# A hand-made order for the first block of a layernorm, attention and routed-FFN kernel

## The chip, the cores and the metric

The kernel runs on one core of one Trainium2 chip. The metric is the time of one execution on the device in microseconds (us). TensorE (PE, with its weight loads PEld), VectorE (DVE), ScalarE (ACT), GpSimd (POOL) and SyncE (SP, which here only issues DMAs) each work through a queue of their own, in order, and wait for one another by semaphores.

## The reference

```python
xn = layernorm(x)                                  # x: 2 x 2048 x 2048, float32
qkv = xn @ Wqkv + bqkv                             # three of 512
attn = softmax(q @ k.T / sqrt(512)) @ v @ Wo + bo
scores = (xn @ Wq.T) @ keys.T                      # 64 experts, 16 kept
gate = one_hot(top16) weighted by softmax(top16)
ffn = ((xn @ A.T) * gate, each 8 times) @ B.T * 2
out = x + attn + ffn
```

## The kernel before, in words

The 4096 tokens are 8 blocks of T = 512, each 4 token tiles of 128. Products are made to near float32 accuracy from a high and a low half: ACT casts a value to its high half (`split_hi`, L127), DVE or POOL subtracts it from the value (`split_lo`, L130), and three matmuls (`PASSES`) make one product. From the second block on, products are formed for pairs of blocks with fewer multiplications, from sums of quarters of the weights ("P1" to "P7"). These sums are made once by POOL (`four_sums`, L541 to L544: four additions), stored to DRAM (`sq_d`, `sv_d`) and read back later. For the feature weights 0 and 2 they are whole tiles of 1024 columns (`set_load`, `set_sums`, `set_out`); for 4, 1, 3 and 5 eight half tiles of 512 columns, called parts (`part_load`, `part_sums`, `part_out`; tile hs, L1169 and L1178). The tables `beside_F` and `beside_V` say behind which step of the features and of the values each part is loaded (L), summed (S_) and stored (O).

`first_block` (from about L320) does the first block's layernorm and its values and router columns (528, in two halves of VH = 264). For each token tile: two rows of x of 1024 columns are loaded (L333); DVE takes statistics (`normal`: L225, L228, L341, L218), POOL the power that gives the reciprocal deviation rs (L219); DVE scales three quarters (L349) and ACT one (L353, L354); PE transposes 16 chunks of 128 x 128 in four groups of four (`turn`, L363), each group into a PSUM bank (acc0, acc1, acc2, acc6); ACT and DVE split the chunks one by one into xh (16 casts, 16 subtractions). Eight weight pieces wh (128 x 2 x 264) are cast on ACT; pieces 2 to 4 are subtracted on POOL, the others on DVE. The sums of token tile t lie in bank acc(3 + t), 48 matmuls each (`mul`, six for each of 8 steps c2). Then `values_out` splits the results into vs and `flush` stores them (L170). In the second half the other 264 columns follow, four banks at once, and beside them the row statistics of the next block (`stats_steps`, whose x rows ACT's queue loads, L243). Then come the features (`features`, 12 weight pieces pw through `fetch`, L622), the values of the second block (`values_by_half`, "Q" and "R"), `third`, and the phases. `whole` (L1140) adds the halves of xh again.

What is issued when is mostly left to a scheduler, which goes by due times; `behind(...)` (`issue_after`) holds an instruction behind named ones.

Of the kernel before, what the change touches and what calls it, by code (L numbers as in the profile page):

```python
# [62 lines left out]
def attn_ffn_kernel(ctx: ExitStack, tc, x, xT, wq, wv, wob, bqk, bv, bo, keysT, out):  # L63
# [114 lines left out]
    XH0 = [s for n in range(3) for s in (GROUPS[3][n + 1], T_SLOTS[n])] + [26, T_SLOTS[3]]  # L178
    XH1 = [s for n in range(3) for s in (GROUPS[2][n + 1], T_SLOTS[4 + n])] + [None, T_SLOTS[7]]

    def split_room(at):
        if at is None:
            return [half(k)([P, T], FR, "xh") for k in (7, 8)]
        t = big(at)([P, 2, T], FR, "xh")
        return [t[:, k, :] for k in range(2)]
# [45 lines left out]
    def stats_steps(i, r, cols, out):  # L231
# [13 lines left out]
        def rows(k):  # L245
            t, c = divmod(k, per)
            if k == 0:
                v["mv"] = const.tile([P, NT, 2], F32, name="mv", bufs=2)
                for n in range(len(r.tags) - 2):
                    load(n)  # L250
# [24 lines left out]

        return [lambda k=k: rows(k) for k in range(NT * per)] + [chain, spread_out]

    mbs = {}
# [40 lines left out]
    def first_block(steps):  # L319
# [3 lines left out]
        xn = [split_room(at) for at in XH0 + XH1]  # L323
        rows, mv = {}, const.tile([P, NT, 2], F32, name="mv", bufs=2)
        rs = const.tile([P, NT], F32, name="rs")
        nm = const.tile([P, NT], F32, name="nm")

# [9 lines left out]

        def normal(t):
            st = const.tile([P, 4, 6], F32, name="st6", bufs=2)
            row_stats(mv[:, t, :], rows[t], 0, st)  # L340
            last["nm"] = nc.vector.tensor_scalar(nm[:, t : t + 1], mv[:, t, 0:1], -1.0, None, ALU.mult)  # L341
            rstd(rs[:, t : t + 1], mv[:, t, 1:2], 1)

        def scale(t):
            for n in range(4):
                c, h = divmod(n, 2)
                v = rows[t][c][:, h * 512 : (h + 1) * 512]
                if n < 3:
                    last["row"] = nc.vector.tensor_scalar(  # L349
                        v, v, mv[:, t, 0:1], rs[:, t : t + 1], ALU.subtract, ALU.mult  # L350
                    )
                else:
                    nc.scalar.activation(v, v, AF.Identity, bias=nm[:, t : t + 1])  # L353
                    last["mul"] = nc.scalar.mul(v, v, rs[:, t : t + 1])  # L354

        def turn(t, g0=0, g1=NCH // 4):
            sl = slice(t * P, (t + 1) * P)
            for g in range(g0, g1):
                pt = acc((0, 1, 2, 6)[g])
                for j in range(4):  # L360
                    c = 4 * g + j
                    k = (c % 8) * P
                    nc.tensor.transpose(pt[:, j * P : (j + 1) * P], rows[t][c // 8][:, k : k + P], ident)  # L363
                for part in range(2):
                    for j in range(4):
                        hi, lo = (xn[4 * g + j][a][:, sl] for a in range(2))
                        pj = pt[:, j * P : (j + 1) * P]
                        if part == 0:
                            split_hi(hi, pj)
                        else:  # L370
                            last["row"] = split_lo(lo, pj, hi)

        r_w0 = Ring(sb, "h0", "h1", "h2", "h3", "B25", "B34", "B35", "B32")

        def mul(ps, wh, t, c2):
            sl = slice(t * P, (t + 1) * P)
            for cc in range(2):
                c = 2 * c2 + cc
                product(
                    ps[:, :VH], lambda a: xn[c][a][:, sl], lambda b: wh[:, b, cc, :],  # L380
                    c == 0, c == NCH - 1,
                )
# [5 lines left out]
        for j in range(25):  # L388
            nc.tensor.matmul(pw, warm[:, :P], warm, start=True, stop=True)
        load(0, 512)  # L390
        normal(0)
        scale(0)

        wh = []

        def piece():
            wh.append(wv_hi(0, len(wh), r_w0))

        def low(n):
            with behind("row", "nm", "mul"):  # L400
                wh[n] = weights_lo(*wh[n], nc.gpsimd if 2 <= n < 5 else None)

        piece()
        piece()
        low(0)
        low(1)
        piece()
        turn(0, 0, 2)
        low(2)
        piece()  # L410
        turn(0, 2, 4)
        low(3)
        piece()
        low(4)
        load(1, 1024)
        for n in range(5, N2):
            piece()
        with behind("row"):
            normal(1)
        with behind("nm"):  # L420
            low(5)
        load(2, 1024)
        ps = []
        for t in range(NT):
            ps.append(acc(3 + t))
            for c2 in range(N2):
                if t + 1 < NT and c2 == 2:
                    scale(t + 1)
                    if t + 2 < NT:
                        with behind("row"):  # L430
                            normal(t + 2)
                if t == 0 and c2 == 4:
                    low(6)
                    low(7)
                    load(3, 1024)
                    constants()
                if t + 1 < NT and c2 == 6:
                    with behind("pe"):
                        turn(t + 1)
                mul(ps[t], wh[c2], t, c2)  # L440
        qr = router_in()
        for t in range(NT):
            with behind("row"):
# [4 lines left out]
        for c2 in range(N2):  # L448
            w = wv_piece(1, c2)
            if c2 == N2 - 1:  # L450
                fetch(0)
            for t in range(NT):
                mul(ps[t], w, t, c2)
# [6 lines left out]
        return xn, qr  # L460
# [77 lines left out]
    def four_sums(w00, w01, w10, w11):  # L538
# [1344 lines left out]
```

## Time and profile before

| | us |
|---|---|
| timed runs: lowest, median, highest of 3 | 2580.51, 2582.38, 2585.69 |
| the profiled execution, span from first to last instruction (the page gives no other time of it) | 2582.2 |
| PE busy in the span | 2556.8 |
| first block, first half: first transposes to the last sum of the fourth token tile | 9.29 to 47.60 |
| first block, second half | 47.60 to 70.83 |
| features | 70.83 to about 137 |
| values of the second block and what follows, up to the last step that the change touches | about 137 to 270 |

A busy share is read together with what ended each idle stretch: the view of waits names who waited for whom, and the timeline gives each instruction's start, its length, and in brackets the idle time before it and who released it. The windows give the busy time of each engine between two moments.

### The profile page before, as it was taken

The numbers are of one execution on the slowest core, as the hardware profiler recorded it, in microseconds if no ns is written. First come the engines' busy times: TensorE is split into PE (matmuls) and PEld (weight loads), VectorE is DVE, ScalarE is ACT, GpSimd is POOL, SyncE is SP. The second block draws the span as 40 slices with busy tenths as digits, with TensorE's granted clock in tenths as the row PEclk, the third lists the DMA queues.
The fourth block names the chain that finished last, engine by engine and source line by source line (L and its number), as shares of the span: only waits on it lengthen the run. The fifth ranks groups of instructions, "written<-read, shape, count | busy, mean of one in ns | idle before, by whom it ended". The sixth has DMA issues, their size and how long they took to land. (4 is left out here: it accounts for less than half of the span.)

```text
span 2582.2 us, 34227 instructions
## 1 busy us (share of the span) xinstructions
PE 2556.8 (99%) x12546; PEld 2159.7 (84%) x12546; DVE 1981.2 (77%) x2692; ACT 926.9 (36%) x1327; POOL 560.8 (22%) x340
## 2 busy tenths in 40 slices
PE   9999999999999999999999999999999999999999
PEld 8897888888888889888887878878878888888887
DVE  7788997867778678777668768688597777797675
ACT  4333333232332323343345446354364222332221
POOL 2382310001000000000000000000013565576654
PEclk9999999999999999999999999999999999999999
DMA  8988964668356673678899798898897554665552
GB/s 297 311 300 276 354 224 144 227 212 274 125 176 225 211 250 120 201 269 270 315 310 309 240 338 278 282 324 290 277 320 265 182 162 157 203 200 179 167 168 101
DMA packets 334297, 615.41 MB, mean 238 GB/s; under 512 B 28409, under 2 KB 151345, under 8 KB 334129
## 3 DMA queue, kind: packets, MB, share of 16 engines
q1 hardware_dynamic: 318864, 583.33, 67.2%
q10 hardware_dynamic: 15264, 29.89, 3.3%
q8 instruction: 99, 1.62, 0.3%
q14 instruction: 70, 0.57, 0.1%
HBM read 457.76 MB, written 155.35 MB: 237 GB/s over the span
## 5 line engine op out<-in xcount | busy, mean ns | idle before, releaser
L135 PE MATMUL acc<-t,pw 128*128 128x512 f32 x3744 | 859.0, 390 | 6.4 <-DVE t L130 4.7
L135 PEld LDWEIGHTS acc<-t,pw 128*128 128x128 f32 x3744 | 699.8, 188 | 153.9 <-DVE t L130 6.4
L1629 PE MATMUL acc<-wb,s 128*128 128x512 f32 x2688 | 609.6, 389 | 0.0
L1629 PEld LDWEIGHTS acc<-wb,s 128*128 128x128 f32 x2688 | 504.4, 188 | 105.0 <-DVE s L130 0.2
L1613 POOL TENSOR_TENSOR xo<-xo,bo_bc 128x512 f32<-128x512 f32 x128 | 213.5, 1675 | 884.5 <-DMA bo_bc<-in_bo 592.3
L127 ACT CAST pw<-pw 128x1024 fp32r<-128x1024 f32 (+1 forms) x218 | 230.5, 1058 | 442.1 <-PE acc L135 287.8
L135 PE MATMUL acc<-ph,vt 128*128 128x512 f32 x1536 | 376.7, 390 | 0.3 <-ACT ot L1474 0.2
L130 DVE TENSOR_TENSOR pw<-pw 128x1024 fp32r<-128x1024 f32 (+1 forms) x218 | 288.7, 1324 | 95.9 <-ACT pw L127 94.3
L135 PEld LDWEIGHTS acc<-ph,vt 128*128 128x128 f32 x1536 | 287.7, 188 | 62.1 <-issue 1.2
L1335 PE MATMUL acc<-qt,kt 128*128 128x512 f32 x1344 | 333.9, 390 | 2.6 <-ACT sp L1345 1.5
L1335 PEld LDWEIGHTS acc<-qt,kt 128*128 128x128 f32 x1344 | 250.9, 188 | 58.9 <-DVE qt L130 2.2
L135 PE MATMUL acc<-pw,t 128*128 128x264 f32 x2400 | 295.9, 285 | 2.9 <-DVE pw L130 0.9
L135 PEld LDWEIGHTS acc<-pw,t 128*128 128x128 f32 x2400 | 294.2, 189 | 5.3 <-ACT pw L127 1.1
L127 ACT CAST s<-xz 128x1024 fp32r<-128x1024 f32 x112 | 118.0, 1054 | 375.1 <-PE acc L1629 300.3
L130 DVE TENSOR_TENSOR s<-xz,s 128x1024 fp32r<-128x1024 f32 x112 | 177.8, 1589 | 41.0 <-ACT s L127 41.0
L130 DVE TENSOR_TENSOR t<-xq,t 128x1024 fp32r<-128x1024 f32 x108 | 141.9, 1321 | 24.3 <-ACT t L127 24.1
L535 POOL TENSOR_TENSOR zt<-zt,g 128x512 f32<-128x512 f32 x28 | 44.6, 1603 | 516.0 <-DMA g<-gd 274.6
L127 ACT CAST t<-xq 128x1024 fp32r<-128x1024 f32 x108 | 113.1, 1051 | 114.1 <-DVE xq L667 59.6
L1618 DVE TENSOR_TENSOR xo<-xo,acc 128x512 f32<-128x512 f32 x128 | 86.9, 680 | 52.1 <-POOL xo L1659 25.2
L127 ACT CAST ph<-sp 128x512 fp32r<-128x512 f32 x128 | 79.4, 620 | 109.4 <-PE acc L135 108.5
L1654 POOL TENSOR_TENSOR xo<-xo,u 128x512 f32<-128x512 f32 x64 | 111.5, 1772 | 21.5 <-DVE u L1652 21.4
L225 DVE BATCH_NORM_STATS2 st<-xs 128x6 f32<-128x512 f32 x128 | 85.0, 683 | 39.5 <-DMA xs<-in_x 39.2
(174 smaller groups left out, 2229.4 us busy)
## 6 DMA issues: line engine op xcount, KB each, us to landing
vt<-v_d SPq DMA_DIRECT2D x128, 512.0 KB, 5.4
kt<-kp_d SPq DMA_DIRECT2D x224, 256.0 KB, 5.7
pw<-sq_d SPq DMA_DIRECT2D x96, 512.0 KB, 4.3
pw<-in_wq SPq DMA_DIRECT2D x72, 512.0 KB, 3.7
xo<-in_x SPq DMA_DIRECT2D x128, 256.0 KB, 3.0
xz<-oz_d SPq DMA_DIRECT2D x64, 512.0 KB, 4.4
out_y<-xo SPq DMA_DIRECT2D x128, 256.0 KB, 2.6
xq<-in_xT SPq DMA_DIRECT2D x56, 512.0 KB, 5.1
```

What stands on the lines that cost most here:

```text
L127: return nc.scalar.copy(hi, src)
L130: return (eng or nc.vector).tensor_tensor(lo, src, raw(hi), ALU.subtract)
L135: last["pe"] = nc.tensor.matmul(ps, st(a_), mv(b_), start=first and n == 0, stop=end and n == 2, skip_group_check=more,)
L225: nc.vector.bn_stats(st[:, parts, :], xt[:, h * 512 : (h + 1) * 512])
L535: nc.gpsimd.tensor_tensor(zt, zt, gx[n], ALU.mult)
L1335: last["pe"] = nc.tensor.matmul(ps, st[:, d, a, :], mv[c][:, d, :], start=not more and d == 0 and i == 0, stop=d == 1 and i == 2, skip_gro ...
L1613: nc.gpsimd.tensor_tensor(xs, xs, bo_bc[q // (NB // 2 * NH), c], ALU.add)
L1618: nc.vector.tensor_tensor(xs, xs, ps, op)
L1629: nc.tensor.matmul(ps, st[a_][:, kk, sl], mv[b_], start=not more and kk == 0 and n == 0, stop=kk == ND - 1 and n == 2, skip_group_check=more,)
L1654: nc.gpsimd.tensor_tensor(xo[q, t, a, 1], xo[q, t, a, 1], v, ALU.add)
```

## The change

The first half of the first block gets a fixed order on each of PE, DVE, ACT and POOL: every instruction issued through `inline` is held behind the one before it on its engine. Within that order: high and low halves of two chunks now share a tile (`pair_rooms` in place of `split_room`), so that one cast and one subtraction treat two chunks (the last pair's low halves stay apart, in two subtractions); each group of transposes is followed by its splits and by a weight cast; weight piece 5 is subtracted on POOL; the fourth group of transposes goes to the bank misc instead of acc6; the transposes of the next tile come one step (six matmuls) later; the three matmuls of a product run in reversed order. The first two parts are loaded behind the last rows of x (`part_load`), summed on POOL between the powers, three sums, three and two, and stored (`part_out`); the tables for the other parts move up by two. The next block's first two rows of x are loaded at the second token tile (`early`). In the second half, the casts and subtractions of four weight pieces come ahead of the results of token tiles 2 and 3. `whole` adds both chunks of a pair at once. `at` gives a chunk of a pair to the matmuls.

```diff
+        early[i] = lambda: [load(n) for n in range(len(r.tags) - 2)]
...
+        tail = {}
+        def inline(key, f, *a, **k):
+            if key in tail:
+                with tc.issue_after(tail[key].ins):
+                    tail[key] = f(*a, **k)
+            else:
+                tail[key] = f(*a, **k)
+            return tail[key]
+        dve = lambda f, *a: inline("dve", f, *a)
+        act = lambda f, *a, **k: inline("act", f, *a, **k)
+        pe = lambda f, *a, **k: inline("pe", f, *a, **k)
+        pool = lambda f, *a: inline("pool", f, *a)
...
         def normal(t):
-            st = const.tile([P, 4, 6], F32, name="st6", bufs=2)
-            row_stats(mv[:, t, :], rows[t], 0, st)
-            last["nm"] = nc.vector.tensor_scalar(nm[:, t : t + 1], mv[:, t, 0:1], -1.0, None, ALU.mult)
-            rstd(rs[:, t : t + 1], mv[:, t, 1:2], 1)
+            dve(nc.vector.bn_aggr, mv[:, t, :], parts[t])
+            ve = const.tile([P, NT], F32, name="ve", bufs=2)
+            dve(nc.vector.tensor_scalar, ve[:, :1], mv[:, t, 1:2], EPS, None, ALU.add)
+            pool(nc.gpsimd.tensor_tensor, rs[:, t : t + 1], ve[:, :1], nhalf[:, :1], ALU.pow)
+            dve(nc.vector.tensor_scalar, nm[:, t : t + 1], mv[:, t, 0:1], -1.0, None, ALU.mult)
...
-        def turn(t, g0=0, g1=NCH // 4):
+                    act(nc.scalar.activation, v, v, AF.Identity, bias=nm[:, t : t + 1])
+                    act(nc.scalar.mul, v, v, rs[:, t : t + 1])
+        turned = {}
+        def turn(t, g):
+            pt = turned[t, g] = acc(g) if g < 3 else misc()
+            for j in range(4):
+                c = 4 * g + j
+                k = (c % 8) * P
+                pe(nc.tensor.transpose, pt[:, j * P : (j + 1) * P], rows[t][c // 8][:, k : k + P], ident)
+        def sides(t, g, part):
             sl = slice(t * P, (t + 1) * P)
-            for g in range(g0, g1):
-                pt = acc((0, 1, 2, 6)[g])
...
-                for part in range(2):
-                    for j in range(4):
-                        hi, lo = (xn[4 * g + j][a][:, sl] for a in range(2))
-                        pj = pt[:, j * P : (j + 1) * P]
-                        if part == 0:
-                            split_hi(hi, pj)
-                        else:
-                            last["row"] = split_lo(lo, pj, hi)
+            for cp in (2 * g, 2 * g + 1):
+                src = turned[t, g][:, (cp % 2) * 2 * P : (cp % 2 + 1) * 2 * P]
+                src = src.rearrange("p (k t) -> p k t", k=2)
+                hi, lo = xn[cp]
+                if part == 0:
+                    act(split_hi, hi[:, :, sl], src)
+                elif isinstance(lo, list):
+                    for k in range(2):
+                        dve(split_lo, lo[k][:, sl], src[:, k, :], hi[:, k, sl])
+                else:
+                    dve(split_lo, lo[:, :, sl], src, hi[:, :, sl])
...
         def mul(ps, wh, t, c2):
             sl = slice(t * P, (t + 1) * P)
             for cc in range(2):
                 c = 2 * c2 + cc
-                product(
-                    ps[:, :VH], lambda a: xn[c][a][:, sl], lambda b: wh[:, b, cc, :],
-                    c == 0, c == NCH - 1,
-                )
+                for n, (a, b) in enumerate(PASSES[::-1]):
+                    pe(
+                        nc.tensor.matmul, ps[:, :VH], at(c, a)[:, sl], wh[:, b, cc, :],
+                        start=c == 0 and n == 0, stop=c == NCH - 1 and n == 2,
+                    )
...
+        def wload(n):
+            for k in range(n):
+                h, cc = divmod(2 * len(ws), HC)
+                ws.append(r_w0([P, 2, VH], F32, "ws"))
+                nc.sync.dma_start(ws[-1], wv[0, h, :, cc : cc + 2, :])
+        def high():
+            n = len(wh)
+            wh.append(r_wh([P, 2, 2, VH], FR, "wh"))
+            last["hi"] = act(split_hi, wh[n][:, 0], ws[n])
+        def low(n):
+            if n in (2, 3, 4, 5):
+                pool(nc.gpsimd.tensor_tensor, wh[n][:, 1], ws[n], raw(wh[n][:, 0]), ALU.subtract)
+            else:
+                dve(split_lo, wh[n][:, 1], ws[n], wh[n][:, 0])
+        wload(5)
+        load(1, 1024)
+        wload(3)
+        load(2, 1024)
+        load(3, 1024)
+        for n in range(2):
+            part_load(n)
...
         normal(0)
+        high()
         scale(0)
...
-        def low(n):
-            with behind("row", "nm", "mul"):
-                wh[n] = weights_lo(*wh[n], nc.gpsimd if 2 <= n < 5 else None)
-        piece()
-        piece()
+        high()
         low(0)
         low(1)
-        piece()
-        turn(0, 0, 2)
-        low(2)
-        piece()
-        turn(0, 2, 4)
-        low(3)
-        piece()
-        low(4)
-        load(1, 1024)
-        for n in range(5, N2):
-            piece()
-        with behind("row"):
-            normal(1)
-        with behind("nm"):
-            low(5)
-        load(2, 1024)
-        ps = []
+        for g in range(4):
+            turn(0, g)
+            sides(0, g, 0)
+            sides(0, g, 1)
+            high()
+            low(2 + g)
+        high()
+        high()
+        stats(1, 0)
+        stats(1, 1)
+        normal(1)
+        low(6)
+        low(7)
+        scale(1)
+        constants()
+        add = lambda *a: pool(nc.gpsimd.tensor_tensor, *a)
+        adds = [ad for n in range(2) for ad in part_adds(n, add)]
+        for ad in adds[:3]:
+            ad()
+        ws1 = []
+        def second_half():
+            h, cc = divmod(2 * len(ws1), HC)
+            ws1.append(r_ws([P, 2, VH], F32, "ws"))
+            last["sp"] = nc.sync.dma_start(ws1[-1], wv[1, h, :, cc : cc + 2, :])
+        for n in range(4):
+            second_half()
+        ps = [acc(3 + t) for t in range(NT)]
         for t in range(NT):
-            ps.append(acc(3 + t))
+            if t == 1:
+                early[1]()
             for c2 in range(N2):
-                if t + 1 < NT and c2 == 2:
-                    scale(t + 1)
+                if t + 1 < NT and c2 == N2 - 1:
+                    for g in range(4):
+                        turn(t + 1, g)
                     if t + 2 < NT:
-                        with behind("row"):
-                            normal(t + 2)
-                if t == 0 and c2 == 4:
-                    low(6)
-                    low(7)
-                    load(3, 1024)
-                    constants()
-                if t + 1 < NT and c2 == 6:
-                    with behind("pe"):
-                        turn(t + 1)
+                        stats(t + 2, 0)
+                    for g in range(3):
+                        sides(t + 1, g, 0)
+                        sides(t + 1, g, 1)
+                    sides(t + 1, 3, 0)
+                    if t + 2 < NT:
+                        stats(t + 2, 1)
+                        normal(t + 2)
+                    sides(t + 1, 3, 1)
+                    if t + 2 < NT:
+                        scale(t + 2)
+                        for ad in (adds[3:6], adds[6:])[t]:
+                            ad()
+                        part_out(t)
                 mul(ps[t], wh[c2], t, c2)
+        last["row"], last["pe"], last["mul"] = tail["dve"], tail["pe"], tail["act"]
         qr = router_in()
-        for t in range(NT):
-            with behind("row"):
+        for t in range(2):
+            with behind("row", "mul"):
+                values_out(0, t, 0, r_ev, qr, ps[t])
+        ahead = []
+        def lead():
+            n = len(ahead)
+            if n < N2:
+                if n + 4 > len(ws1) and len(ws1) < N2:
+                    second_half()
+                w = r_wh([P, 2, 2, VH], FR, "wh")
+                with behind("row", "mul"):
+                    last["hi"] = split_hi(w[:, 0], ws1[n])
+                    last["dve"] = split_lo(w[:, 1], ws1[n], w[:, 0])
+                ahead.append(w)
+        for n in range(4):
+            lead()
+        for t in range(2, NT):
+            with behind("row", "mul"):
                 values_out(0, t, 0, r_ev, qr, ps[t])
         flush()
...
-            w = wv_piece(1, c2)
+            lead()
             if c2 == N2 - 1:
                 fetch(0)
             for t in range(NT):
-                mul(ps[t], w, t, c2)
+                mul(ps[t], ahead[c2], t, c2)
+            last["pe"] = tail["pe"]
...
+    def four_adds(w00, w01, w10, w11, tt=None):
+        tt = tt or nc.gpsimd.tensor_tensor
+        return (w11, w00, w10, w01), [
+            lambda: tt(w11, w10, w11, ALU.add),
+            lambda: tt(w10, w00, w10, ALU.subtract),
+            lambda: tt(w00, w11, w00, ALU.subtract),
+            lambda: tt(w01, w01, w00, ALU.subtract),
+        ]
...
-    RINGS = (0, 0, 2, 1, 0, 2, 1, 0)
+    RINGS = (1, 0, 0, 0, 2, 1, 0, 2)
...
-        6: [lambda: set_sums(2)] + x11[0] + [L[0]],
-        7: [S_[0]] + x11[1][:2],
+        6: [lambda: set_sums(2)] + x11[0] + [L[2]],
+        7: [S_[2]] + x11[1][:2],
         8: x11[1][2:],
-        9: [lambda: set_out(2), O[0]] + q_[:2],
-        10: [L[1]] + b0 + q_[2:3],
-        11: [S_[1]] + q_[3:] + [L[2]],
+        9: [lambda: set_out(2), O[2]] + q_[:2],
+        10: [L[3]] + b0 + q_[2:3],
+        11: [S_[3]] + q_[3:] + [L[4]],
...
     beside_V = {
-        ("Q", 0, 0): [S_[2], L[3]],
-        ("Q", 0, 1): [S_[3], O[1]] + t3[:2],
-        ("Q", 1, 0): [O[2], L[4]] + t3[2:],
-        ("Q", 1, 1): [S_[4], L[5]] + r_[:2],
-        ("R", 0, 0): [O[3], S_[5]] + r_[2:],
-        ("R", 0, 1): [O[4], L[6]],
-        ("R", 1, 0): [O[5], L[7], S_[6], lambda: state.update(q=router(qr1))] + b1[:2],
-        ("R", 1, 1): [S_[7]] + b1[2:],
-        0: [O[6], lambda: state.update(w=choose(state["q"]))] + t2[:2],
-        1: [O[7]] + p6[:1] + t2[2:],
+        ("Q", 0, 0): [S_[4], L[5]],
+        ("Q", 0, 1): [S_[5], O[3]] + t3[:2],
+        ("Q", 1, 0): [O[4], L[6]] + t3[2:],
+        ("Q", 1, 1): [S_[6], L[7]] + r_[:2],
+        ("R", 0, 0): [O[5], S_[7]] + r_[2:],
+        ("R", 0, 1): [O[6]],
+        ("R", 1, 0): [O[7], lambda: state.update(q=router(qr1))] + b1[:2],
+        ("R", 1, 1): b1[2:],
+        0: [lambda: state.update(w=choose(state["q"]))] + t2[:2],
+        1: p6[:1] + t2[2:],
```

## The prediction

> **What bounds the kernel now.** I read the page first: busy shares, then the windows by stage, then who PE waits for.
>
> ```profile
> PE 2556.8 (99%) x12546; PEld 2159.7 (84%) x12546; DVE 1981.2 (77%) x2692; ACT 926.9 (36%) x1327; POOL 560.8 (22%) x340
> ```
>
> PE is idle for 2582.2 − 2556.8 = 25.4 us of the span. Whatever this change can win lies in that, plus matmuls that run stretched. The windows (columns: length, then busy time and count of PE, PEld, DVE, ACT, POOL, granted clock, DMA share, GB/s) say where:
>
> ```profile
> 9.29:47.60 38.31, 33.51 (x259) 32.05 (x258) 30.57 (x105) 21.53 (x85) 11.15 (x8) 0.96 0.79 274
> 47.60:70.83 23.23, 23.23 (x193) 23.23 (x192) 20.70 (x36) 8.56 (x15) 5.00 (x3) 1.00 0.92 331
> 70.83:160.00 89.17, 89.17 (x485) 77.44 (x484) 70.99 (x82) 29.15 (x41) 51.73 (x25) 1.00 0.90 305
> 160.00:270.00 110.00, 102.68 (x539) 87.24 (x538) 92.49 (x127) 39.29 (x53) 41.11 (x23) 1.00 0.87 294
> ```
>
> The first half of the first block ends at 47.60 and loses 4.8 us to idle PE. The second half and the features lose nothing; the stages from 160 to 270 lose 7.3. Past that the change moves nothing. Inside the first block, from the waits and the timeline:
>
> ```profile
> PE acc L135 <- DVE xh L130: 2.5, 3, 1.4
> PE acc L135 <- DVE wh L130: 1.9, 1, 1.9
> ...
> 18.51 0.88 PE L135 MATMUL acc<-wh,xh 128*128 128x264 f32 x5 [1.89 <-DVE wh L130]
> 18.91 1.46 DVE L349 TENSOR_SCALAR xs<-xs,mv,rs 128x512 f32<-128x512 f32 x3 [0.46 <-POOL rs L219]
> 38.21 3.25 DVE L130 TENSOR_TENSOR xh<-acc,xh 128x128 fp32r<-128x128 f32 x16 [2.31 <-ACT xh L127]
> 41.52 3.68 PE L135 MATMUL acc<-wh,xh 128*128 128x264 f32 x28 [1.38 <-DVE xh L130]
> ```
>
> PE waits 1.89 us for the subtraction of weight piece 5, which stands behind the statistics of the second token tile. It waits 1.38 us at 41.52, exactly until the sixteenth xh subtraction ends (38.21 + 3.25 = 41.46): the sums of the fourth token tile use bank acc6, where the fourth group of transposes still lies.
>
> **The order, without the half tiles.** Unstretched, 240 matmuls from 41.52 to 70.83 go at 0.122 us each; 16 transposes take 1.66 (36.77 to 38.43).
>
> First token tile: until DVE's last xh at about 14.8 nothing gets quicker. DVE: one pair instruction lies between the rows 128x248 (three in 1.05, 0.35 each) and 128x264 (432 ns alone), so 8 pairs are 2.9 us where 16 singles take 3.25. ACT: 8 casts at no more than 0.37 (128x248) against 16 in 2.81. Both are hidden here behind the weight casts now put between them. Then statistics 2.46, small ones 0.4, pieces 6 and 7 at 0.65 each, and the scaling ends near 20.4 (20.37 before); the second tile's transposes end near 22.0 (before 22.15). But piece 5 goes to POOL and piece 6 comes early, so 6 matmuls are left instead of 12: the tile ends at 22.75. Three rounds of 42 matmuls (5.13), 16 transposes (1.66) and 6 matmuls (0.73), the last with 48 (5.86) and no transposes, end at 43.7. DVE's round (statistics 2.46, scaling 1.46, pairs 2.9, small 0.5: 7.3 us) just fits PE's 7.5. The acc6 wait goes, as that group moves to misc. **47.6 − 43.7 = 3.9 won.** If the clock drops again as it did (0.83 from 20 to 30, after the 1.89 us idle), that costs up to 1.7; PE still pauses about 1.5 us near 18 in my schedule, so I take 0.8.
>
> **The half tiles inside it.** Eight loads go on SP's queue behind the last rows of x. Those are issued up to 12.2 and land after 7.5 (median): 19.7. Four loads are 1.05 MB, 2.5 us at the 412 GB/s seen there: 22.3. The two x rows of the next block, moved from 42.6 to about 16 on ACT's queue, are another 1.05 MB in between: 24.8 at most. I take 23.6. Three sums follow on POOL at 1.29 each (the shortest rows), and behind them in the same queue stands the power of the third tile's variance (0.57): ready at 28.0 (26.7 to 29.2). PE comes to these transposes at 22.75 + 5.13 = 27.9, their third group 0.8 later needs the third scaling, and three scalings take 1.46: the power must be there by 27.2. So the wait is 0.8 (0 to 2.0).
>
> While the scaling of the third and fourth tiles runs on DVE, POOL works on the next sums. The trace has no such meeting, but it has neighbours:
>
> ```profile
> 125.70 4.89 DVE L1140 TENSOR_TENSOR xq<-xh 128x512 f32<-128x512 f32 x8
> ...
> 128.82 6.38 POOL L541 TENSOR_TENSOR hs<-hs 128x512 f32<-128x512 f32 x1 [15.47 <-DMA hs<-in_wq]
> ...
> 139.86 4.54 DVE L667 TENSOR_TENSOR xq<-xq 128x1024 f32<-128x1024 f32 x2
> ...
> 173.10 0.40 DVE L302 TENSOR_TENSOR vs<-acc,xv 128x248 f32<-128x248 f32 x1
> ```
>
> Columns: start, length, engine, line. Two DVE instructions with both inputs in SBUF took 2.27 each beside POOL's sums, 1.2 without: about 1.1 more, most of one sum. At 128.8 it was POOL that waited, and DVE lost nothing. One with an input in PSUM takes 0.40 with or without POOL; statistics at 14.84, one SBUF input, also ran at 2.46 beside it. Scaling has one SBUF input, like the statistics, but goes faster (0.485 against 0.615 for 512), so it may read as the pairs do. Bounds: 0 to two sums of 1.1 at the third tile, 0 to 1.2 at the fourth (one sum is absorbed). I take 1.1: one sum that gets in first, since DVE started only 0.04 us after the power ended (8.07 to 8.11).
>
> The Trainium skill (SBUF — State Buffer, section "SBUF: two separate sides") states that a VectorE instruction in a two-port mode, or one with two SBUF inputs, and a GpSimd instruction lock each other out for a whole instruction, whoever starts first. The L667 row agrees, the row at 128.8 does not quite; by the rule alone the upper bound would hold at both tiles, and the first block would come out 1.1 us slower than before.
>
> Sum for the first block: −3.9 + 0.8 (clock) + 0.8 (power) + 1.1 (scaling) = **−1.2**, from −3.9 to +3.2.
>
> **What costs nothing, and what hides it.** SP's weights for the features are now queued behind the stores of the second part, so behind POOL's last sum (about 40) instead of 22.9: their casts run at 62, that is 20 us of cover. The early x rows cost ACT's queue two issues of 0.4, where ACT idles 1.67. Splits of later weights ahead of two results: PE waits for nothing from 47.6 to 160, so they gain nothing; the two results come 2.6 us later, and their banks are next used after 70. If that cover went, PE would wait those 2.6.
>
> **The later stages.** Two of eight parts leave the stages up to 190: eight sums (2.15 each by the median), and 4.2 MB of loads and stores. No subtraction need wait for these sums after 174. Six PE waits remain to be won there: 0.47, 0.66, 1.72, 2.40, 0.61 and 1.45, together 7.3. The first two lie before the part sums that are gone; the third (204.3) is a weight subtraction in DVE's backlog right after them; the last three come from value sums and late loads, untouched. I take 1.5 won. On the loss side, the two sets of 1024-wide sums now fall later, beside DVE's splits before 70: two collisions of 2.3, against the 2.5 us that DVE has free there: 2.1 lost. Bounds −7.3 to +2.1.
>
> **Total:** −1.2 − 1.5 = −2.7. The page gives a span of 2582.2 for the profiled execution, and no other time of it; the median of the timed runs is 2582.38, so I add nothing: **2579.7 us**. Ends of the terms: −11.2 and +5.3.
>
> **Rivals.**
> - Full gain, 0.28. The power comes in time, scaling is not held, the clock stays up (−3.9), and the relief from 174 on removes three of the late waits, about 4: 2574.5. For it: DVE free of sums after 174; DMA share only 0.48 from 30 to 40, where the new traffic goes. Against: those waits have other sources too.
> - Swallowed, 0.20. The first block wins 2 to 4 us, and PE then waits longer at 161 to 204, where DVE (92.5 of 110 busy), POOL and DMA set the pace: 2582. For it: PE is already held there; against: much of what DVE does there is released by PE.
> - Slower, 0.17. The power for the third tile stands on POOL behind three sums that stand behind late half tiles, and PE waits at that tile's transposes. With full holding at both tiles (3.4) the win is gone once the first part lands after 23.3; without any, after 26.7. At 24.8 with holding: 2.0 + 3.4 − 3.9 = +1.5, with the clock drop +3.2, and with the 2.1 before 70 +5.3: 2584 to 2588. For it: POOL runs strictly in order; against: the row at 128.8.
> - The forecast, 0.35.
>
> That the instructions do not stand as the change says is excluded: the built order of POOL's queue shows three sums, power, three sums, power, two sums.
>
> **Chances.** 0.2% is 5.2 us, about what a measurement of this kernel can tell from no change. Faster by more: the full gain, 0.28. Slower by more: the worse two thirds of its case, 0.12. Within: 0.60. The range leaves out the best third of the full gain and the last tenth at the other end: 2573.0 to 2587.7.
>
> **What would show it.** First half over near 45 to 46.5 instead of 47.6; no PE wait on xh before the fourth tile; 6 matmuls after each group of transposes. Right or wrong on the sums: the start of the third tile's scaling (28.0) and its length (1.46 alone, 2.6 with one sum, 3.7 with two). Later: the wait at 204 gone, the one at 226 still there. A first part landing after 25, or a new PE wait between 47 and 160, would make the prediction wrong.

## The result, and the profile after

The changed kernel takes 2587.89 us (median of 22 runs, 2584.53 to 2592.33), the kernel before 2583.38 us beside it (22 runs). The ratio is 1.0020, 95% interval 1.0014 to 1.0026: **slower by 0.2%, about 5 us**, where 2.7 us less had been forecast. The profiled execution has a span of 2589.7 us and a time of 2591.5 us, 3.6 above the median; so a time is 1.8 us above its span, and before's 2582.2 stands for about 2584.0.

The same four windows as for before, with the same columns:

```profile
9.29:47.60 38.31, 30.50 (x216) 28.39 (x217) 31.10 (x70) 18.32 (x50) 17.63 (x15) 0.87 0.80 283
47.60:70.83 23.23, 23.23 (x194) 23.23 (x193) 13.87 (x29) 8.56 (x17) 0.38 (x1) 1.00 0.91 326
70.83:160.00 89.17, 86.62 (x447) 73.94 (x446) 76.09 (x88) 27.15 (x40) 47.43 (x22) 0.98 0.86 298
160.00:270.00 110.00, 104.73 (x584) 92.04 (x582) 86.89 (x119) 41.28 (x55) 37.09 (x21) 0.98 0.80 274
```

In the first window PE is busy for 30.50 us instead of 33.51, at a clock of 0.87 instead of 0.96; in the third, where before lost nothing, 2.55 us are gone; the last one wins 2.05. PE's waits, longest groups first:

```profile
PE acc L340 <- issue: 5.5, 2, 5.3
PE acc L135 <- ACT yv L1050: 3.8, 1, 3.8
PE misc L603 <- DVE wk L595: 2.2, 1, 2.2
PE acc L135 <- DVE t L130: 1.7, 2, 0.9
```

The wait at acc6 (1.4) is gone, and of the 1.89 for the subtraction of piece 5 only 0.27 is left (0.85 for piece 6 stands beside it). A wait of 5.3 us has come in, put down to "issue". The timeline says what it is:

```profile
14.53 10.90 SPq L1281 DMA_DIRECT2D hs<-in_wq  x8
...
26.35 3.96 POOL L340 TENSOR_TENSOR hs<-hs 128x512 f32<-128x512 f32 x3 [7.78 <-DMA hs<-in_wq]
30.26 0.55 POOL L340 TENSOR_TENSOR rs<-ve,nhalf 128x1 f32<-128x1 f32 x1
30.85 4.30 DVE L340 TENSOR_SCALAR xs<-xs,mv,rs 128x512 f32<-128x512 f32 x3 [5.07 <-POOL rs L340]
32.43 1.09 PE L340 MATMUL acc<-ident,xs 128*128 128x128 f32 x4 [5.27 <-issue]
...
36.84 7.57 PE L340 MATMUL acc<-wh,xh 128*128 128x264 f32 x48
...
40.70 3.36 DVE L340 TENSOR_SCALAR xs<-xs,mv,rs 128x512 f32<-128x512 f32 x3
```

Read it from the top. The first part lands at 26.35. Three sums follow on POOL, behind them the power of the third token tile (30.26), behind that DVE's scaling (30.85), which had waited 5.07, and behind that PE's transposes, at 32.43 instead of 27.16, when PE was free. The scaling takes 4.30 us beside the next three sums (1.46 alone), the fourth tile's 3.36. The 48 matmuls after the pause take 7.57 us instead of about 6.1: the clock has dropped. The fourth tile's matmuls begin at 45.91, where before had them at 41.52.

Why the first part landed so late can be read from SP's issues and from what the queues moved between 19.7, when the prediction had the rows of x in, and 26.35 (q1 is SP's queue, q10 ACT's; the columns are packets, MB, share of the 16 engines):

```profile
14.53 3.57 SPq L1281 DMA_DIRECT2D hs<-in_wq  x4
...
21.98 3.45 SPq L1281 DMA_DIRECT2D hs<-in_wq  x4
...
q1 hardware_dynamic: 937, 1.72, 69.1%
q10 hardware_dynamic: 237, 0.84, 32.1%
```

The four loads of the first part were issued by 18.10, so the last of them was under way for over 8 us. In the 6.65 us from 19.7 on 2.57 MB passed, 387 GB/s: the first part itself (1.05 MB), 0.84 MB of the next block's early rows of x, and on SP's queue 0.67 MB more than the first part holds, which is the second part's own loads, issued from 21.98 on.

PE's delay against before, at five places of the profiled executions (us): +4.4 at the fourth tile's matmuls, +5.6 at the start of the features, +9.7 at that of the values, +14.6 at the third stage, +7.5 at the end (the medians differ by 4.5; this execution is one of the longer ones).

### The profile page after: what moved, and what is told of

Read it like the earlier page. It is cut to its first block, busy times and chain, and to the rows that moved or that the text cites. A ratio compares the mean times of both kernels' runs of the same rounds, so it can differ in the third digit from the quotient of the medians.

```text
span 2589.7 us, 34186 instructions
## 1 busy us (share of the span) xinstructions
PE 2561.6 (99%) x12546; PEld 2163.7 (84%) x12546; DVE 1977.7 (76%) x2656; ACT 924.3 (36%) x1295; POOL 547.2 (21%) x341
## 5 line engine op out<-in xcount | busy, mean ns | idle before, releaser
L1729 POOL TENSOR_TENSOR xo<-xo,bo_bc 128x512 f32<-128x512 f32 x128 | 205.5, 1613 | 890.3 <-DMA bo_bc<-in_bo 590.8
L130 DVE TENSOR_TENSOR s<-xz,s 128x1024 fp32r<-128x1024 f32 x112 | 170.7, 1527 | 42.3 <-ACT s L127 42.3
L1461 ACT COPY sp<-acc 128x512 f32<-128x512 f32 x128 | 74.7, 585 | 105.3 <-PE acc L1451 103.0
```

What stands on the lines that cost most here:

```text
L130: return (eng or nc.vector).tensor_tensor(lo, src, raw(hi), ALU.subtract)
L1461: last["copy"] = nc.scalar.copy(*ops)
L1729: nc.gpsimd.tensor_tensor(xs, xs, bo_bc[q // (NB // 2 * NH), c], ALU.add)
```

## The experiments

My theory after this result: the order alone wins, the sums inside it cost more than that. Rivals: the order or the pairs cost it; only the late power does, not the sums beside the scaling; the later stages do. Of each run I give the ratio to before, measured beside it (0.001 is 2.6 us) and the start of the fourth tile's matmuls (before 41.52, after 45.91).

**Order alone.** The first block's loads, sums and stores of parts 0 and 1 leave, tables and buffers become those of before:

```diff
-        for n in range(2):
-            part_load(n)
...
-        for ad in adds[:3]:
-            ad()
...
-                        for ad in (adds[3:6], adds[6:])[t]:
-                            ad()
-                        part_out(t)
...
-    RINGS = (1, 0, 0, 0, 2, 1, 0, 2)
+    RINGS = (0, 0, 2, 1, 0, 2, 1, 0)
```

> The kernel after, with the two parts (half tiles) taken out of the first block again: their loads, sums and stores stand in the tables of the features and values where the kernel before has them, and their buffers are the ones of before. The hand-made order, the pairs, the early x rows and the earlier splits of the second half stay. My theory (the sums cost it, the order wins): the third token tile's scaling starts near 28.0 or earlier and is 1.46 long, the fourth's too, no PE wait above 1.5 us after 22, the first half is over at 43.7 to 45 (47.6 before, 52.6 after), and the time is 3 to 9 us below the kernel after, so 2579 to 2584. Rival 'the order or the pairs cost it': the first half is still over after 48 and the time stays within 1 us of the kernel after. Rival 'the later stages cost it' (earlier loads and splits in the second half, the wait at 107): the first half is over by 45 but the values and third stage start as late against it as in the kernel after, and the time is above the kernel before.

Ratio 0.9996 (0.9987 to 1.0005), median 2580.50. The fourth tile begins at 36.64; no wait of PE from 20 to 160 is longer than 0.25 us:

```profile
26.07 1.45 DVE L340 TENSOR_SCALAR xs<-xs,mv,rs 128x512 f32<-128x512 f32 x3
...
29.05 6.09 PE L340 MATMUL acc<-wh,xh 128*128 128x264 f32 x48
...
36.64 6.58 PE L340 MATMUL acc<-wh,xh 128*128 128x264 f32 x52
...
160.31 8.06 PE L135 MATMUL acc<-pw,t 128*128 128x264 f32 x63 [2.85 <-ACT yv L1041]
...
223.89 4.56 DVE L130 TENSOR_TENSOR t<-xq,t 128x1024 fp32r<-128x1024 f32 x2
226.26 1.21 PE L135 MATMUL acc<-t,pw 128*128 128x512 f32 x3 [4.35 <-DVE t L130]
```

The order wins 4.9 us in the first block (3.9 was the forecast for it), so the rival of the order falls. Most of it is given back: the total is about 1 us below before, and the interval includes no change. PE comes earlier to 160 and 226 and waits longer there. At 226 before has the same wait:

```profile
223.95 4.58 DVE L130 TENSOR_TENSOR t<-xq,t 128x1024 fp32r<-128x1024 f32 x2
226.32 1.65 PE L135 MATMUL acc<-t,pw 128*128 128x512 f32 x6 [2.40 <-DVE t L130]
```

Two splits on DVE take 4.6 us beside a value sum on POOL, at the same moment whenever PE arrives.

**Sums and scaling, two by two.** Three kernels separate the late power from the sums beside the scaling. "Later" sums none ahead of the third power, three behind the issue of its scaling, five behind the fourth's, and stores both parts after that. "Held" puts a tiny addition on POOL ahead of the sums, which reads the last column that DVE scaled:

```diff
-        for ad in adds[:3]:
-            ad()
...
-                        for ad in (adds[3:6], adds[6:])[t]:
-                            ad()
-                        part_out(t)
+                        for ad in (adds[:3], adds[3:])[t]:
+                            ad()
+                        if t == 1:
+                            part_out(0)
+                            part_out(1)
```

```diff
+        def hold(t):
+            gt = const.tile([P, NT], F32, name="gt", bufs=2)
+            pool(nc.gpsimd.tensor_tensor, gt[:, :1], rows[t][1][:, 511:512], nhalf[:, :1], ALU.add)
...
                         scale(t + 2)
+                        hold(t + 2)
```

Later alone:

> The kernel after, with no sum ahead of the third token tile's power: three sums after the issue of the third tile's scaling, five after the fourth's, and both parts are stored after that. This takes away the late power at the third tile and keeps the sums beside the scalings. If late power is the main cost: power near 23, the third scaling starts there, PE's 5.3 us wait falls to under 1.5, the first half ends at 46 to 48. If the sums beside the scaling are the main cost: the half tiles land after that scaling is over, so the third tile isn't held; the fourth scaling is still held by about 1.9 and is 3.4 long. My theory: about 4 us of the first half's 5.0 come back, end near 47 to 48, time 2581 to 2586. Rival 'later stages': the first half is over by 48 and the total stays at 2587 to 2589.

Held alone:

> The kernel after, with one tiny addition on POOL behind each scaling of the third and fourth tile that reads the last column scaled by DVE, so that no sum can run beside the scaling; the three sums stay ahead of the third tile's power. This takes away the holding and keeps the late power: power near 30.8, both scalings 1.46 long (4.30 and 3.36 in the kernel after). My theory: the first half ends 2.8 + 1.0 earlier than after at most, some of it lost to the clock: 49 to 50.5, time 2584 to 2587. If holding isn't what makes the scaling long, it stays near 4 and 3.4.

Both:

> Both edits: no sum ahead of the third tile's power, and no sum beside a scaling. My theory: power near 23, scalings 1.46 long, no PE wait above 1.5 us from 22 to 48, first half over at 43.7 to 45.5, at least 6 us ahead of the kernel after; the sums run in POOL's gaps and are done by about 42. Time 2577 to 2583 if the later stages keep it, 2583 to 2587 if they lose it again (rival 'later stages').

| | scalings, us | fourth tile begins | ratio to before | interval |
|---|---|---|---|---|
| after | 4.30, 3.36 | 45.91 | 1.0020 | 1.0014 to 1.0026 |
| held | 1.46, 1.45 | 43.26 | 1.0022 | 1.0012 to 1.0031 |
| later | 3.50, 4.28 | 40.19 | 1.0007 | 0.9998 to 1.0017 |
| later and held | 1.45, 1.45 | 36.79 | 1.0005 | 0.9996 to 1.0014 |

The window from 26 to 46 of the four, in the order of the table (a line for each kernel):

```profile
26.00:46.00 20.00, 14.09 (x91) 13.16 (x90) 13.58 (x24) 5.87 (x16) 11.45 (x10) 0.74 0.61 192
```

```profile
26.00:46.00 20.00, 15.78 (x114) 15.60 (x113) 11.68 (x33) 8.55 (x27) 11.48 (x12) 0.83 0.63 201
```

```profile
26.00:46.00 20.00, 17.25 (x140) 16.24 (x139) 17.89 (x36) 10.07 (x30) 11.14 (x9) 1.00 0.67 205
```

```profile
26.00:46.00 20.00, 20.00 (x169) 20.00 (x169) 16.10 (x41) 11.49 (x33) 11.60 (x12) 1.00 0.79 261
```

PE's busy time rises from 14.09 to 20.00, and the clock is down only in the two kernels with the late power. Taking the late power away brings 3.4 and 4.4 us of the total; taking the holding away brings nothing that can be measured, though it brings 2.7 and 3.4 us in the first block. I had been wrong for "later" on one point: there too the third scaling is held (3.50), since the half tiles land at 26.45, half a microsecond after it starts. With both mended the first block is as quick as with the order alone (36.79 and 36.64), and the total is still 0.9 thousandths (2.3 us) above it, with intervals that overlap (0.9996 to 1.0014 and 0.9987 to 1.0005).

**Where that rest lies.** In the last kernel PE waits 1.9 us at 68.9 (feature weights, subtracted at 67.25) and 4.5 at 167.6 (yv, ACT's copies of sums in the values stage). SP's queue:

```profile
36.28 6.03 SPq L1300 DMA_DIRECT2D sq_d<-hs  x5
42.41 1.35 SPq L498 DMA_DIRECT2D ws<-in_wv  x3
...
47.45 1.94 SPq L737 DMA_DIRECT2D pw<-in_wq  x2
```

The stores stand there until the last sum is done at 42; the last four of the second half's weight loads and most of the feature weights stand behind them. Four kernels tested that and the other parts of the change. First, no additions at all in the kernel after (both loops `for ad in ...: ad()` removed), so that the half tiles are stored unsummed:

> The kernel after without the eight additions of the two parts in the first block (work left out: the loaded half tiles are stored unsummed, so these weights' sums are not formed); their loads and stores stay where they are. Theory 'GpSimd's additions cost it, directly (power, scaling) and by holding SP's queue until they are done': the first half is over at 42.5 to 43, the stores are issued near 30 instead of up to 43, no PE wait near 69 and 105, and with the later stages relieved of two parts the time is 2576 to 2580. Rival 'the traffic of the parts costs it, added up or not' (8 loads and 8 stores on SP's queue ahead of the weights): the waits near 69 and 105 are there as in the run with the sums later and held, and the time is 2582 to 2585.

Ratio 0.9980 (0.9972 to 0.9989). But its profiled execution (2582.5, the longest of its 11) has the same waits as the kernel with the sums later and held: 2.5 at 69, 1.0 at 99.8, 3.8 at 167, and a span only 1.2 us shorter, where the medians differ by 6. The trace doesn't show those 5 us, and the weights that later stages read are other numbers; I draw nothing from it.

Second, the order alone with the second half's splits where before had them (`values_out` for all four tiles first, each piece split in its own step):

> The order-only kernel with one more part of the change undone: in the second half, no split comes ahead of the results; the results of all four token tiles are taken out first, and each weight piece is split in its own step. Theory: these splits had cover, the time stays within 1.5 us of the order-only run (2580.5), and the second half starts at most 2.6 us later. Rival 'the splits ahead let the second half run through': a PE wait of 1 to 3 us at the start of the second half near 42.5.

Ratio 0.9989 (0.9980 to 0.9998), median 2580.04, no wait at the second half: these splits had cover, as forecast. Third, the same without the early x rows (`early[1]()` removed):

> The order-only kernel with the splits ahead of results and the early x rows undone: the hand-made order and the pairs alone. Theory (early rows cost and bring nothing): first half over at 42.5 to 43, time within 1.5 us of the run with the splits back (2580.0). Rival 'the early rows relieve the statistics in the second half': PE waits of 1 to 3 us between 60 and 100, and 2582 to 2584.

Ratio 0.9995 (0.9986 to 1.0004), a PE wait of 1.19 at 47.4 for a weight piece: within what can be told apart, nothing. Fourth, the order alone with ACT's copies xv and yv ahead of the casts behind them:

> The order-only kernel with one edit far from the first block: ACT's copies of the sums in the values stage (xv, yv) stand ahead of the casts that wait for later loads. It tests why the 4 to 5 us won in the first block did not reach the total. Theory 'ACT's queue holds the bank': the wait of 2.85 at 160 goes. If what follows has slack, the time falls by 2 to 3 us, to 2578; rival 'from 200 on other queues set the pace' (DVE and GpSimd at the splits near 202 and 226): the waits at 202 and 226 grow by what was won, and the time stays at 2580 to 2581.

Ratio 0.9994 (0.9985 to 1.0002). The wait at 160.3 (2.85) is gone and one of 6.5 stands at 163.0, for a split t on DVE; those at 202 and 226 (1.60, 4.35), which the rival let grow, shrink to 0.4 and nothing. A wait taken away here comes back at the next queue, and the time is the same.

**The stores elsewhere.** Behind the second half's weights and the first feature loads on SP:

```diff
+            last["sp"] = last["w8"] = nc.sync.dma_start(ws1[-1], ...)
...
         fetch(1)
+        with behind("sp", "w8"):
+            for n in range(2):
+                part_out(n)
```

> The run with the sums later and held, and the stores of both parts now queued on SP behind the second half's weight loads and the first feature loads. Theory 'SP's queue, standing at stores that wait for sums, delays the loads behind them': the features' weights are issued before 32 instead of from 42 to 56, the PE wait of 1.9 at 69 is gone, statistics and the row of means (mb) come earlier and so the wait for wk near 100 goes; the time falls by 2 to 4 us, to 2580 to 2582, while the wait at 167 for yv stays (it has other causes). Rival 'the stages from 120 on are paced by GpSimd's remaining sums': the early waits go, but the wait at 167 grows by as much and the time stays at 2583 to 2584.

Ratio 1.0014 (1.0005 to 1.0023). Worse:

```profile
57.38 0.36 ACT L127 CAST vs<-acc 128x248 fp32r<-128x248 f32 x1 [2.46 <-DMA sq_d<-hs]
...
58.24 24.04 PE L340 MATMUL acc<-wh,xh 128*128 128x264 f32 x174 [11.07 <-DVE vs L130]
```

A first result's tile vs waits for a store of a half tile, and PE waits 11.07 us for the bank that this result holds. The half tiles of parts 0 and 1 (rings 1 and 0: B27, B28, B29, B9) lie in the very buffers of the first results (`r_ev`). Issued by ACT, part 0 ahead of the fourth tile's casts:

> The run with the sums later and held, with the two parts' eight stores issued by ACT instead of SP (part 0's four sums behind the third scaling and its stores ahead of the fourth tile's casts, part 1's behind the first four casts of the second half's weights). Buffers, loads and tables are as in the kernel after. Theory 'SP's queue stood at these stores': the features' weights are issued near 30, the wait at 69 (1.9) and the one near 100 go, and 2 to 4 us come back: 2580 to 2582. Rival 'the results' tiles share buffers with the half tiles and wait for the stores themselves, whoever issues them': casts of vs still wait for the stores, and a PE wait stands between 42 and 60. Rival 'swallowed later': waits go, and the wait near 167 grows by as much; time 2583 to 2584.

Ratio 1.0017 (1.0008 to 1.0026). The same coupling from the other end:

```profile
33.63 1.96 ACTq L340 DMA_DIRECT2D sq_d<-hs  x4
...
47.26 0.36 ACT L127 CAST vs<-acc 128x248 fp32r<-128x248 f32 x1 [9.24 <-DMA sq_d<-hs]
...
48.55 0.59 PE L340 MATMUL acc<-wh,xh 128*128 128x264 f32 x1 [5.16 <-ACT wh L127]
```

The stores are issued from 33.6 on, but SP's weight loads, now issued from 30.7, travel beside them (that this is what slows the stores was not tested); the cast waits until 47.2, and the weight casts behind it on ACT with it.

**The parts' place in the tables.** With the sums later and held, the six other parts one place later (before's places 1 to 6, where the change uses places 0 to 5):

```diff
-    RINGS = (1, 0, 0, 0, 2, 1, 0, 2)
+    RINGS = (1, 0, 0, 2, 1, 0, 2, 1)
...
-        10: [L[3]] + b0 + q_[2:3],
-        11: [S_[3]] + q_[3:] + [L[4]],
+        10: [L[2]] + b0 + q_[2:3],
+        11: [S_[2]] + q_[3:] + [L[3]],
```

> The run with the sums later and held, with the six other parts one place later in the tables of features and values (so that the two places won lie one ahead and one behind, where the kernel after leaves both behind). Theory 'from 120 to 175 SP's queue, GpSimd's sums and the splits on DVE set the pace together, and two parts fewer there relieve it only where they are taken from': the wait at 167 (4.5) falls below 2 and waits near 200 to 226 stay below 2; time 2579 to 2582. Rival 'the wait at 167 comes from ACT's order alone': it stays at 4 to 5, and the time stays at 2583 to 2585.

Ratio 0.9989 (0.9980 to 0.9998), 4 us less than without (1.0005, 0.9996 to 1.0014; the intervals just overlap): the wait near 167 falls from 4.47 to 1.86 (at 164.1). One of 2.59 stands at 226.7, where less than 2 was forecast. The same tables in the changed kernel itself, with nothing else:

> The kernel after with nothing changed but the place of the six other parts in the tables (spread, one place later); sums, powers and scalings in the first block are as in the kernel after. If the place of the parts costs the same there as in the run with held sums (3.7): the first half is over near 52.6 as before, and the time is 2583 to 2585, 3 to 5 below the kernel after. If the late first block hides it: 2586 to 2588.

Ratio 1.0017 (1.0008 to 1.0026): 0.8 us at most likely, and within both intervals nothing. The time, 2586.40, is the one forecast for the case that the late first block hides it. Stores on ACT and tables together:

> Stores on ACT and parts spread, together. If the two relieve different waits: no PE wait above 1 us from 22 to 160, 2576 to 2580. If what is won earlier is swallowed by the stages from 120 on: 2581 to 2584, as the better of the two.

Ratio 1.0012 (1.0004 to 1.0021): the better tables, and still the 5.2 us for the buffers. So the buffers had to be tested alone. Part 0 moves to B6 and B7, part 1 to H1 to H4, with the tables spread:

```diff
+            if n == 0:
+                t = big(6 + fh)([P, 2, T], F32, "hs")
...
+            elif n == 1:
+                v = [half(1 + 2 * fh + ch)([P, T], F32, "hs") for ch in range(2)]
```

> The run with the sums later and held and the parts spread (2580.2), with the two early parts in buffers of their own (B6, B7, H1 to H4, free until 72) instead of those that the first results' tiles (vs) use. Theory 'results wait for the stores of the sums because they share buffers, and everything behind them on ACT waits too': the casts of vs no longer wait for stores (2.19 and 1.06 at 42.7 and 45.2 in the run without own buffers); with the stores still ahead of the weights on SP's queue the PE wait at 69 stays at 1 to 2, time within 1 us of 2580.

Ratio 0.9993 (0.9984 to 1.0002); no vs waits for a store any more, and a wait of 2.7 stays at 69. Then the stores late once more, as in the kernel with the 11 us:

> Own buffers, parts spread, sums later and held, and the stores queued on SP behind the second half's weights and the first feature loads. With shared buffers that order made PE wait 11 us at 58. Theory 'the 11 us came from the shared buffers alone': no PE wait above 1 us from 22 to 160, features begin near 66.5; the time is 2577 to 2580 if the stages from 160 pass on 2 us, 2580 to 2582 if they swallow it again. Rival 'the order of the stores itself is bad': a PE wait of 5 us or more between 45 and 70 and over 2584.

Ratio 0.9989 (0.9981 to 0.9998), median 2580.30. The 11 us are gone, PE runs through from 20 to 95, and from 160 to 300 it is busy for 137.08 us (before 132.68):

```profile
160.00:190.00 30.00, 29.46 (x215) 27.97 (x214) 27.00 (x28) 9.85 (x16) 19.47 (x11) 1.00 0.89 306
190.00:250.00 60.00, 57.84 (x253) 46.87 (x252) 50.08 (x82) 20.96 (x29) 15.99 (x8) 1.00 0.77 256
250.00:300.00 50.00, 49.78 (x220) 40.78 (x219) 48.10 (x56) 17.30 (x18) 11.97 (x7) 1.00 0.97 350
```

This version, the one with spread tables, and the order with the splits back are each 0.0011 below before, with intervals that end at 0.9998: a narrow margin for the best three of fourteen kernels that do all the work. They can't be told from one another: two parts inside the first block bring nothing measurable even where they cost nothing there.

## Why the prediction was wrong

- **The order, −3.9:** right in the first block, and more: −4.9 with the order alone. The acc6 wait is gone, pieces 5 and 6 come with 0.27 and 0.85 us of wait instead of 1.89, and the splits ahead and the early rows cost nothing that can be measured, as forecast. But the sum carried this win to the end whole. With the order alone about 1 of the 4.9 us is left there (0.9996), and longer waits at 160 and 226 (2.85 and 4.35 us, before 0.47 and 2.40) take much of the rest; the rival "swallowed" (0.20) had named this.
- **The landing of the first part, 23.6 (24.8 at most): the step that failed first.** Measured is 26.35. By 19.7 SP's queue had moved 5.86 MB, as much as the weights and rows ahead of the parts hold, as assumed. What I had wrong is the traffic behind them: at most 2.1 MB at 412 GB/s, of which I counted the early rows half. It was 2.57 MB at 387 GB/s, since the second part's own loads were issued before the first had landed and took 0.67 MB of it; the sum had no term for them. No run loads the first part alone, so how early it would then land stays open.
- **The late power, 0.8 (0 to 2.0): the step that failed with it.** The power was ready at 30.81 instead of 28.0, and PE, which came at 27.16, a little earlier than the 27.9 assumed, paused 5.27 us. With the scaling not held the pause is still 4.22, so 1 us of it belongs to the holding. Taking the late power away brings the fourth tile forward by 5.7 and 6.5 us, more than the order won there, and 3.4 to 4.4 us of the total.
- **The clock, 0.8 (0 to 1.7):** the 48 matmuls behind the wait took 1.5 us more, and from the first transpose to the first matmul it was 4.41 us instead of 1.67 (order alone), 0.6 of it small waits: about 3.6 in all, outside the bounds. Without the late power the clock stays at 1.00 from 26 to 46; after the pauses of 5.27 and 4.22 us it is 0.74 and 0.83 there. The Trainium skill (TensorE: Matmul & The Clock Gate, Part 1) says that an idle window of about 3.4 us halves the clock and a busy one gives it back. These two pauses agree with it; shorter ones don't all: the clock also fell after 1.89 us in the kernel before (0.83 from 20 to 30) and after 2.17 us at 107 in the changed kernel (0.72 over the next 6 us), and not after 2.40 us at 226 in the kernel before (1.00). In this case a pause below 3.4 us is no safe one.
- **Scaling held, 1.1 (0 to 3.4):** 2.84 and 1.90 longer, together 4.7. At 1.36 us a sum that is two sums let in at the third tile and one and a half at the fourth; my "one sum gets in first" was too small. But the total doesn't show it: the held kernel has the same ratio. The step's size was wrong and its weight for the time, too.
- **The later stages, −1.5 (−7.3 to +2.1):** the relief came (after 190 PE loses 0.8 us up to 300, where before lost 6.2), but was paid for ahead of it: 2.2 at 107, 4.7 from 160 to 176. I had asked only what two parts fewer free, not what six parts sooner load: one place later in the tables is worth about 4 us in the kernel with held sums. In the changed kernel itself the two can't be separated.
- **The rival "slower"** (0.17) named this place, with the point from which it decides: a win is gone once the first part lands after 26.7 without holding, 23.3 with it. It landed at 26.35 with holding, and the time is inside that rival's 2584 to 2588. Its weight was too low because I took the landing from the middle of my bounds.

What stays open: why the kernel without additions is 5 us quicker in the median than its trace shows, and how far one profiled execution stands for a median at all: from 300 to 2570, where the kernels do the same work, PE's busy time ranges from 2260.0 to 2264.5 us over these traces.

## What to carry to other kernels

Before filling an engine's idle time in an in-order queue, look at what stands behind the filler: a 0.55 us power behind three sums behind a load decided this change. Put fillers behind the short instruction that the critical path waits for, count every load that travels beside the one you wait for, those queued behind it too, and check whose buffers the filler borrows. And a win in an early stage is worth only what the next stages, paced by several queues at once, let through.

## What the runs showed of the hardware

DVE's scaling with one input in SBUF (tensor_scalar, 128x512) is held by POOL's additions: three take 4.30 instead of 1.46 us, POOL's own additions staying at 1.3 to 1.4 each. The opposite is there too. In the kernel with the sums later and held, one POOL addition, 2.40 us at 89.77, lasted 16.87: DVE ran two-input instructions back to back and at full speed until 119.85, and the addition ended 2.25 us later (two of DVE's rows from that stretch below it):

```profile
105.23 16.87 POOL L653 TENSOR_TENSOR pw<-pw 128x1024 f32<-128x1024 f32 x1 [9.64 <-DVE pw L130]
...
108.42 2.35 DVE L762 TENSOR_TENSOR xq<-xq,mb 128x1024 f32<-128x1024 f32 x2
110.69 2.35 DVE L763 TENSOR_TENSOR xq<-xq,mb 128x1024 f32<-128x1024 f32 x2
```

The rule of the Trainium skill weighed in the prediction (SBUF — State Buffer, "SBUF: two separate sides": whoever starts first holds the other for a whole instruction) fits the scaling, not this row: here POOL waited through a dozen instructions of DVE. So the two are not alike in these rows. DVE's instructions without a gap kept POOL out to the end; POOL's three additions, also without a gap (30.78 to 34.86), let one scaling in at a time, since PE's transposes, each group of which needs one more, start at 32.43, 33.88 and 35.25. That is how I read the rows; no run tested it.
